# A decoder layer's shared expert: its last units in blocks of 512 tokens instead of 256

## The chip, the cores and the metric

The kernel runs on one core of a Trainium2 chip. The metric is device time in microseconds (us) of one execution. The engines are named as in the profile: PE (TensorE matmuls), PEld (TensorE weight loads), DVE (VectorE), ACT (ScalarE), POOL (GpSimd) and SP (SyncE, which issues most DMA transfers).

## The reference

One pre-norm decoder layer over x of 2 x 2048 tokens with 512 channels, all in float32:

```python
x = x + attn(layernorm(x))       # "attention" against two fixed matrices of 512 x 512, squared ReLU
x = x + xattn(layernorm(x))      # cross attention, 16 heads, 128 context rows, masked softmax
x = x + ffn(layernorm(x))

def ffn(h):                      # h: 4096 x 512
    shared = (silu(h @ sg) * (h @ su)) @ sd          # 512 -> 1024 -> 512, all tokens
    logits = h @ gate_w                              # 32 experts, the best one for each token
    e, s = argmax(logits), sigmoid(max(logits))
    xs = h * s
    routed = (silu(xs @ rg[e]) * (xs @ ru[e])) @ rd[e]
    return shared + routed
```

The change concerns `shared` alone, and of its 1024 hidden units only the last 256.

## The kernel before

Float32 products are made of three matmuls each. Every operand is split into a high part (a cast by ACT to the reduced type `fp32r`) and a low part (the difference, by DVE or POOL), and `three` lists low x high, high x low and high x high. So every weight or activation that comes from memory as `raw` costs one ACT cast and one DVE subtraction (`split`, L94 and L97) before PE can use it.

The layer goes through four stages. `stage0` is the first attention, `stage1` the cross attention and the routing scores. `stage1` also writes the normalised input of the feed-forward part, transposed and already split, to memory as `zT`: index 0 is the high part, index 1 the low part, then 128 partitions, 4 chunks k of 128 channels, and 4096 tokens in an order of its own (`place`). `shared` computes the first 768 hidden units of the shared expert. `routed` then computes the routed experts, and between their blocks the shared expert's last 256 units, which the class `Rest` holds.

`routed` sorts the experts by the number of their tokens into 32 ranks with fixed capacities:

```python
CAP = [448, 384] + [256] * 5 + [192] * 4 + [128] * 13 + [64] * 8
```

Its order takes one rank of over 128 rows, then one of 64 and one of 128, and so on, and two of 128 when those of 64 are used up. A rank is cut into blocks of 256, 128 or 64 rows. The list `blocks` mixes these with the blocks of `Rest`. Before the change, a `Rest` block has 256 tokens. The first stands ahead of everything, and one more follows each rank whose capacity isn't 128, until 15 are placed (behind ranks 0 to 7 and the seven ranks of 64 between them).

For block i the program writes, in this order: `prepare` of block i+2 (the gather of an expert's rows by POOL, or `Rest.load` by SP), the load of the next rank's gate weights (if this is the rank's last block), `first` (the gate product, or half of gate and up for 256 rows), the transposes of block i+1's rows, the transposes of block i-1's hidden rows, the load of the up weights, `second`, then `third` of block i-1 (its down product, and the store that adds it to the output) and the load of the down weights. The framework plans the final order of each engine from this order and its own estimate of the times, and each engine then follows its plan in order.

What limits the room: the pool W has 45 pieces of 128 x 512. The weights of `Rest` hold 12 of them and a rank's gate and up weights 32. The down weights use tags A and B. Raw weights pass through 6 slots of the pool `raw` and 8 of tag F. Tag E has 4 slots and serves the input z of `Rest`. PSUM has eight banks, two each under the tags P1 to P4. The tag I has two slots, for the rows v that go to the output. The names in the profile are L1107 (load of z), L1118 (gate and up of `Rest`), L1126, L1133, L1147 (down of `Rest`), L1150 and L1151 (copy and adding store of its rows), L1190 (raw weights), L1202 (gather), L1209, L1228 and L1308 (transposes), L1238 (blocks of 64 and 128 rows), L1293 and L1328 (blocks of 256 rows), L1336 (adding scatter of an expert's rows) and L1007 and L975 (the last of `shared`).

Of the kernel before, what the change touches and what calls it, by code (L numbers as in the profile page):

```python
# [8 lines left out]
F32 = mybir.dt.float32  # L9
FR = mybir.dt.float32r  # L10
# [4 lines left out]
A = mybir.AluOpType  # L15
AF = mybir.ActivationFunctionType
# [5 lines left out]
T = 4096  # L22
C = 512
E = 32
# [5 lines left out]
CAP = [448, 384] + [256] * 5 + [192] * 4 + [128] * 13 + [64] * 8  # L30
# [11 lines left out]
def f32(ap):  # L42
    return ap.bitcast(F32)


class Ctx:
# [4 lines left out]
    def __init__(self, tc, stack):  # L51
        self.tc, self.nc = tc, tc.nc
        enter = stack.enter_context
        self.c = enter(tc.tile_pool(name="c", bufs=1))
        self.sm = enter(tc.tile_pool(name="sm", bufs=3))
        self.raw = enter(tc.tile_pool(name="raw", bufs=6))
        self.W = enter(tc.tile_pool(name="W", bufs=45))
        self.a = enter(tc.tile_pool(name="a", bufs=1))
        self.ps = enter(tc.tile_pool(name="ps", bufs=2, space=PSUM))
# [29 lines left out]
def split(g, hi, lo, src, lo_engine=None, hi_engine=None):  # L89

    if isinstance(lo_engine, cycle):
        lo_engine = next(lo_engine)
    if hi_engine is None:
        g.nc.scalar.copy(hi, src)  # L94
    else:
        hi_engine.tensor_copy(hi, src)
    g.low = (lo_engine or g.nc.vector).tensor_tensor(lo, src, f32(hi), A.subtract)  # L97
# [22 lines left out]
def part(w, k, c):  # L120

    return w[k][c // 4][:, c % 4 * 128:c % 4 * 128 + 128]
# [40 lines left out]
def three(terms):  # L163

    (wh, wl), (xh, xl) = terms
    return (wl, xh), (wh, xl), (wh, xh)
# [199 lines left out]
def place(t):  # L366

    at = t // 4 * 4 + t % 2 * 2 + t % 4 // 2
    return slice(at * 256, at * 256 + 256)
# [723 lines left out]
class Rest:  # L1093


    def __init__(self, g, zT, out):
        self.g, self.zT, self.out = g, zT, out
        self.Z, self.S, self.H = {}, {}, {}

    def load(self, b):  # L1100
        g, nc = self.g, self.g.nc
        z = []
        for c in range(2):
            z.append([])
            for i in range(2):
                v = g.tile("E", "z", FR, (128, 2, 256))
                nc.sync.dma_start(f32(v[:]), self.zT[i, :, 2 * c:2 * c + 2, place(b)])  # L1107
                z[c].append(v)
        self.Z[b] = z

    def product(self, b, which, tag):
        g, nc = self.g, self.g.nc
        p = g.bank(tag, which, (128, 2, 256))
        for i in range(2):
            n = 0
            for k in range(4):
                for w, x in three((g.rest[which], self.Z[b][k // 2])):
                    nc.tensor.matmul(p[:, i, :], part(w, k, i), x[:, k % 2, :], start=n == 0, stop=n == 11)  # L1118
                    n += 1
        return p  # L1120

    def gate(self, b):
        g, nc = self.g, self.g.nc
        p = self.product(b, "g", "P2")
        s = g.tile("G", "s", F32, (128, 2, 256))
        nc.scalar.activation(s[:], p[:], AF.Silu)  # L1126
        self.S[b] = s

    def up(self, b):
        g, nc = self.g, self.g.nc  # L1130
        p = self.product(b, "u", "P3")
        s = self.S.pop(b)
        nc.vector.tensor_tensor(s[:], p[:], s[:], A.mult)  # L1133
        hh, hl = g.tile("C", "hh", FR, (128, 2, 256)), g.tile("D", "hl", FR, (128, 2, 256))
        split(g, hh[:], hl[:], s[:])
        self.H[b] = hh, hl
        del self.Z[b]

    def down(self, b):
        g, nc = self.g, self.g.nc  # L1140
        h = self.H.pop(b)
        for j in range(2):
            o = g.bank("P1", "d")
            n = 0
            for k in range(2):
                for w, y in three((g.rest["d"], h)):
                    nc.tensor.matmul(o[:], y[:, k, j * 128:(j + 1) * 128], w[k][0], start=n == 0, stop=n == 5)  # L1147
                    n += 1
            v = g.tile("I", "v")
            nc.scalar.copy(v[:], o[:])  # L1150
            nc.gpsimd.dma_start(self.out[b * 256 + j * 128:b * 256 + j * 128 + 128, :], v[:], accum_op=A.add)  # L1151

def routed(g, xs, rest, plan, idx, wg, wu, wd, out):
    nc = g.nc
    big = [r for r in range(E) if CAP[r] > 128]
    one = [r for r in range(E) if CAP[r] == 128]
    half = [r for r in range(E) if CAP[r] == 64]
    order = []  # L1160
    while big or one or half:
        few = half[:1] + one[:1] if half else one[:2]
        order += big[:1] + few
        big, one, half = big[1:], [r for r in one if r not in few], half[1:]
# [90 lines left out]
    def gate(b, r, m):  # L1255
        S[b] = []
        for n, p in enumerate(up_product(b, r, "g", "P2")):
            if m == 64:
                if n == 0:
                    S[b].append(g.tile("G", "s"))  # L1260
                both(S[b][0], p, n)
            else:
                s = g.tile("G", "s")
                nc.scalar.activation(s[:], p[:], AF.Silu)
                S[b].append(s)
        if m == 64:
            nc.scalar.activation(S[b][0][:], S[b][0][:], AF.Silu)

    def up(b, r, m):
        if m == 64:  # L1270
            u = g.tile("D", "u")
            for n, p in enumerate(up_product(b, r, "u", "P3")):
                both(u, p, n)
            s = S[b][0]
            nc.vector.tensor_tensor(s[:], u[:], s[:], A.mult)
            return
        for s, p in zip(S[b], up_product(b, r, "u", "P3")):
            nc.vector.tensor_tensor(s[:], p[:], s[:], A.mult)

    def hidden(b, r, part):  # L1280
        if part == 0:
            HT[b] = []
        for q in (2 * part, 2 * part + 1):
            o = []
            for which, tag in (("g", "P2"), ("u", "P3")):
                p = g.bank(tag, which, (128, 2, 256))
                for i in range(2):
                    cols = slice((2 * q + i) % 4 * 128, (2 * q + i) % 4 * 128 + 128)
                    n = 0
                    for k in range(4):  # L1290
                        piece = 2 * k + q // 2
                        for w, x in three((W[r][which], X[b][k // 2])):
                            nc.tensor.matmul(p[:, i, :], w[piece][:, cols], x[:, k % 2, :], start=n == 0, stop=n == 11)  # L1293
                            n += 1
                o.append(p)
            s = g.tile("G", "s", F32, (128, 2, 256))
            nc.scalar.activation(s[:], o[0][:], AF.Silu)
            nc.vector.tensor_tensor(s[:], o[1][:], s[:], A.mult)
            hh, hl = g.tile("C", "hh", FR, (128, 2, 256)), g.tile("D", "hl", FR, (128, 2, 256))
            split(g, hh[:], hl[:], s[:])  # L1300
            HT[b].append((hh, hl))
# [35 lines left out]
                                         in_=v[rows], in_offset=None, bounds_check=T - 1, oob_is_err=False, compute_op=A.add)  # L1337


    left = [(b, None, 256) for b in range(T // 256)]  # L1340
    blocks = [left.pop(0)]
    for r in order:
        at = 0
        while at < CAP[r]:
            m = next(m for m in (256, 128, 64) if at + m <= CAP[r])
            blocks.append((BASE[r] + at // 128, r, m))
            at += m
        if CAP[r] != 128 and left:
            blocks.append(left.pop(0))
    blocks += left  # L1350
    nxt = dict(zip(order, order[1:]))
# [7 lines left out]

    def first(b, r, m):  # L1360
        if r is None:
            rest.gate(b)
        elif m < 256:
            gate(b, r, m)
        else:
            hidden(b, r, 0)

    def second(b, r, m):
        if r is None:
            rest.up(b)  # L1370
        elif m < 256:
            up(b, r, m)
        else:
            hidden(b, r, 1)
# [7 lines left out]
    def turn_x(b, r, m, *tag):  # L1382
        if r is not None:
            turn(b, r, m, *tag)

    def turn_hidden(b, r, m):
        if r is not None:
            turn_h(b, r, m)
# [5 lines left out]
    for w in "gud":  # L1394
        load(order[0], w)
    for i, block in enumerate(blocks):
        b, r, m = block
        last = r is not None and (i + 1 == len(blocks) or blocks[i + 1][1] != r)
        if i + 2 < len(blocks):
            prepare(*blocks[i + 2])  # L1400
        if last and r in nxt:
            load(nxt[r], "g")
        first(*block)
        if i + 1 < len(blocks):
            turn_x(*blocks[i + 1])
        if i > 0:
            turn_hidden(*blocks[i - 1])
        if last and r in nxt:
            load(nxt[r], "u")
        second(*block)  # L1410
        if i > 0:
            third(*blocks[i - 1])
            r = blocks[i - 1][1]
            if r != block[1] and r in nxt:
                load(nxt[r], "d")
# [144 lines left out]
```

## Time and profile before

| what | value |
|---|---|
| median of 3 runs | 2699.37 us (2699.36 to 2700.18) |
| profiled execution, its own time | 2698.85 us |
| its span, first to last instruction | 2697.1 us |
| mean granted clock of PE | 0.996 |
| instructions of PE, busy share | 14629, 98% |
| gate and up of `Rest` (L1118) | 768 matmuls of 128 x 256, from 1789.8 us on; the last starts at about 2471 us |
| down of `Rest` (L1147) | 192 matmuls of 128 x 512 |
| loads of z for `Rest` (L1107) | 64 of 256 KB by SP |
| adding stores of `Rest` (L1151) | 32 of 256 KB by POOL |

A row of the profile's groups gives the line of the code, the engine, the operation, the output and the inputs, the shape, the count, the busy time and the mean time of one. A row of the timeline gives the start, the time and, in brackets, how long the engine stood idle before it and what ended that. Matmuls are pipelined, so one starts before the one ahead of it has ended, and the distance from start to start says more than the time of a row. A row of the windows gives a stretch, each engine's busy time and number of instructions in it, the granted clock, the busy share of the DMA engines and their GB/s.

### The profile page before, as it was taken

Reading aid. Unit: us, or ns where it says so; the run is one execution under the profiler, and the core shown is the slowest. Engines: PE = TensorE matmul, PEld = TensorE weight load, DVE = VectorE, ACT = ScalarE, POOL = GpSimd, SP = SyncE. Lnnn points to the kernel's source line nnn. Section 1 sums busy time; section 2 is a strip of 40 time slices with the busy share of each in tenths; the row PEclk is TensorE's granted clock in tenths of the full one; section 3 lists DMA queues with packets and bytes.
Section 4 is the critical chain, followed back from the end, with each engine's and each line's share of the span. In section 5 each row is a group of like instructions: output and inputs, shape, how many; then the busy total and the mean of one; then the engine's idle time right before and its main releaser. Section 6 shows DMA issues by size and latency. Waiting matters only on the chain. (4 is left out here: it accounts for less than half of the span.)

```text
span 2697.1 us, 47526 instructions
## 1 busy us (share of the span) xinstructions
PE 2639.6 (98%) x14629; PEld 2274.4 (84%) x14629; DVE 2033.8 (75%) x4559; ACT 1873.8 (69%) x4152; POOL 1129.3 (42%) x911
## 2 busy tenths in 40 slices
PE   7999999999999999999999999999999999999998
PEld 5878888887879999999987878778889898888886
DVE  7777777777777888888876596564776777778995
ACT  7788787888778877877874333333666777767885
POOL 5576566666654334444440547620122122212321
PEclk9999999999999999999999999999999999999999
DMA  4112112212020224232249846673899899999994
GB/s 154 32 63 87 55 67 81 77 43 83 30 86 27 87 76 138 96 108 90 102 158 327 273 140 239 223 214 109 260 287 276 279 302 292 299 280 291 325 324 142
DMA packets 269409, 446.68 MB, mean 166 GB/s; under 512 B 33536, under 2 KB 77568, under 8 KB 269152
## 3 DMA queue, kind: packets, MB, share of 16 engines
q1 hardware_dynamic: 254464, 416.46, 45.6%
q0 software_dynamic: 14688, 27.17, 5.1%
q8 instruction: 116, 1.90, 0.3%
q14 instruction: 141, 1.16, 0.1%
HBM read 348.83 MB, written 96.64 MB: 165 GB/s over the span
## 5 line engine op out<-in xcount | busy, mean ns | idle before, releaser
L97 DVE TENSOR_TENSOR rl<-raw,rh 128x512 fp32r<-128x512 f32 x768 | 488.2, 683 | 90.6 <-ACT rh L94 64.0
L94 ACT CAST rh<-raw 128x512 fp32r<-128x512 f32 x768 | 438.3, 621 | 141.6 <-DMA raw<-in_rg 98.2
L97 POOL TENSOR_TENSOR pl<-p,ph 128x512 fp32r<-128x512 f32 x320 | 411.4, 1297 | 264.3 <-ACT ph L94 210.0
L349 ACT ACTIVATE rl<-s 128x512 f32<-128x512 f32 x512 | 293.2, 604 | 38.2 <-PE s L345 30.6
L1336 POOL DMA_INDIRECT out_dram<-v,idx x46 | 114.2, 2483 | 463.6 <-ACT v L1334 368.7
L470 POOL TENSOR_TENSOR e<-e,ri 128x512 f32<-128x512 f32 x128 | 132.8, 1043 | 305.8 <-DVE ri L468 159.4
L353 DVE TENSOR_TENSOR p<-s,rl 128x512 f32<-128x512 f32 x320 | 215.1, 683 | 41.7 <-ACT rl L349 39.1
L94 ACT CAST ph<-p 128x512 fp32r<-128x512 f32 x320 | 199.2, 626 | 60.1 <-DVE p L353 57.4
L467 ACT ACTIVATE e<-e,mn 128x128 f32<-128x128 f32 x512 | 199.9, 392 | 27.9 <-DVE mn L462 26.7
L345 PE MATMUL s<-qh,kwl 128*128 128x512 f32 x512 | 205.5, 403 | 6.4 <-DVE p L353 3.1
L309 PE MATMUL o<-pl,vwh 128*128 128x512 f32 x512 | 203.1, 397 | 2.2 <-POOL pl L97 2.2
L353 DVE TENSOR_TENSOR s<-s,rl 128x512 f32<-128x512 f32 x192 | 133.3, 694 | 91.2 <-ACT rl L349 90.8
L309 PE MATMUL o<-ph,vwl 128*128 128x512 f32 x512 | 200.9, 394 | 1.0 <-ACT ph L94 1.0
L345 PE MATMUL s<-ql,kwh 128*128 128x512 f32 x512 | 200.3, 391 | 0.0
L345 PE MATMUL s<-qh,kwh 128*128 128x512 f32 x512 | 200.1, 391 | 0.0
L309 PE MATMUL o<-ph,vwh 128*128 128x512 f32 x512 | 199.6, 390 | 0.0
L975 PE MATMUL gu<-z,swh 128*128 128x512 f32 x504 | 158.3, 392 | 0.0
L440 PE MATMUL q<-yh,wql 128*128 128x256 f32 x512 | 147.3, 288 | 1.5 <-ACT yh L94 0.6
L97 DVE TENSOR_TENSOR pl<-s,ph 128x512 fp32r<-128x512 f32 x192 | 131.1, 683 | 21.1 <-ACT ph L94 18.6
L440 PE MATMUL q<-yh,wqh 128*128 128x256 f32 x512 | 146.3, 286 | 0.0
L440 PE MATMUL q<-yl,wqh 128*128 128x256 f32 x512 | 145.9, 285 | 0.0
L345 PEld LDWEIGHTS s<-qh,kwl 128*128 128x128 f32 x512 | 96.6, 189 | 33.1 <-DVE p L353 8.6
(361 smaller groups left out, 7958.0 us busy)
## 6 DMA issues: line engine op xcount, KB each, us to landing
raw<-in_rg SPq DMA_DIRECT2D x256, 256.0 KB, 5.4
raw<-in_ru SPq DMA_DIRECT2D x256, 256.0 KB, 5.4
raw<-in_rd SPq DMA_DIRECT2D x256, 256.0 KB, 5.3
z<-zT SPq DMA_DIRECT2D x116, 256.0 KB, 5.6
b<-x SPq DMA_DIRECT2D x40, 256.0 KB, 3.0
raw<-in_sgu SPq DMA_DIRECT2D x39, 256.0 KB, 4.2
swh<-wS SPq DMA_DIRECT2D x36, 256.0 KB, 4.9
swl<-wS SPq DMA_DIRECT2D x36, 256.0 KB, 4.9
```

What stands on the lines that cost most here:

```text
L94: g.nc.scalar.copy(hi, src)
L97: g.low = (lo_engine or g.nc.vector).tensor_tensor(lo, src, f32(hi), A.subtract)
L309: nc.tensor.matmul(o[:], w, y[:], start=kt == 0 and n == 0, stop=kt == 15 and n == 2)
L345: nc.tensor.matmul(s[:], w, y[:], start=n == 0, stop=n == 2)
L349: m0 = nc.scalar.activation(r[:], s[:], AF.Relu)
L353: m1 = nc.vector.tensor_tensor(p[:], s[:], r[:], A.mult)
L440: nc.tensor.matmul(o[:, i, :], part(w, k, p), y[k // 2][:, k % 2, :], start=n == 0, stop=n == 11)
L467: nc.scalar.activation(e[:, hs], e[:, hs], AF.Exp, bias=mn[:, h:h + 1], scale=-1.0, accum_out=su[:, h:h + 1])
L470: nc.gpsimd.tensor_tensor(e4, e4, ri[:].unsqueeze(2).to_broadcast([128, 4, 128]), A.mult)
L975: nc.tensor.matmul(o[:], y, z, start=(at, x) not in begun, stop=j == 1 and m == 2, skip_group_check=True)
L1336: nc.gpsimd.indirect_dma_start(out=out, out_offset=bass.IndirectOffsetOnAxis(ap=idx[rows, b + j:b + j + 1], axis=0), in_=v[rows], in_offse ...
```

## The change

`Rest` now has blocks of 512 tokens: 8 in place of 16. The input of a block is eight tiles of 128 x 512 (four chunks k, each with a high and a low part). `load` fetches the four high parts into the four slots of E and the first low part into a piece of W. The method `hidden` replaces `gate` and `up` and has two halves. The first half goes over the high parts: each meets the low and the high part of the gate and up weights, for both groups of 128 hidden units, in four PSUM banks that are open at the same time (P2 twice, P3 twice). As soon as a high part is used up, POOL fetches one of the other three low parts into its slot. The second half goes over the low parts, which meet the high parts of the weights, and then evicts the four banks: Silu, multiplication in PSUM, split. `down` makes four row groups of 128 tokens in a row, in P1 and P4 by turns.

The first block stands ahead of everything as before, but the transposes of the block after it now follow its second half. The other seven stand behind the ranks with a capacity over 128 and under 384, so behind ranks 2 to 8.

```diff
+    def part(self, b, i, k, engine, spare=False):
+        v = self.g.piece("z") if spare else self.g.tile("E", "z", FR)
+        engine.dma_start(f32(v[:]), self.zT[i, :, k, b * 512:(b + 1) * 512])
+        return v
+
     def load(self, b):
+        sp = self.g.nc.sync
+        self.Z[b] = [self.part(b, 0, k, sp) for k in range(4)] + [self.part(b, 1, 0, sp, True)]
+
+    def hidden(self, b, half):
         g, nc = self.g, self.g.nc
-        z = []
-        for c in range(2):
-            z.append([])
+        z = self.Z[b]
+        if half == 0:
+            self.S[b] = o = {}
             for i in range(2):
-                v = g.tile("E", "z", FR, (128, 2, 256))
-                nc.sync.dma_start(f32(v[:]), self.zT[i, :, 2 * c:2 * c + 2, place(b)])
-                z[c].append(v)
-        self.Z[b] = z
+                for which, tag in (("g", "P2"), ("u", "P3")):
+                    o[which, i] = g.bank(tag, which)
+        o = self.S[b]
+        for k in range(4 * half, 4 * half + 4):
+            if 0 < k < 4:
+                z.append(self.part(b, 1, k, nc.gpsimd))
+            for i in range(2):
+                for which in "gu":
+                    hi, lo = (part(w, k % 4, i) for w in g.rest[which])
+                    for n, w in enumerate((lo, hi) if k < 4 else (hi,)):
+                        nc.tensor.matmul(o[which, i][:], w, z[k][:], start=k == 0 and n == 0, stop=k == 7, skip_group_check=True)
+        if half == 0:
+            return
+        self.H[b] = []
         for i in range(2):
...
+            s, p = g.tile("G", "s"), o["u", i]
+            nc.scalar.activation(s[:], o["g", i][:], AF.Silu)
+            nc.vector.tensor_tensor(p[:], p[:], s[:], A.mult)
+            hh, hl = g.tile("C", "hh", FR), g.tile("D", "hl", FR)
+            split(g, hh[:], hl[:], p[:])
+            self.H[b].append((hh, hl))
 
     def down(self, b):
         g, nc = self.g, self.g.nc
         h = self.H.pop(b)
-        for j in range(2):
-            o = g.bank("P1", "d")
+        for s in range(4):
+            o = g.bank(("P1", "P4")[s % 2], "d")
             n = 0
             for k in range(2):
-                for w, y in three((g.rest["d"], h)):
-                    nc.tensor.matmul(o[:], y[:, k, j * 128:(j + 1) * 128], w[k][0], start=n == 0, stop=n == 5)
+                for w, y in three((g.rest["d"], h[k])):
+                    nc.tensor.matmul(o[:], y[:, s * 128:(s + 1) * 128], w[k][0], start=n == 0, stop=n == 5)
                     n += 1
             v = g.tile("I", "v")
             nc.scalar.copy(v[:], o[:])
-            nc.gpsimd.dma_start(self.out[b * 256 + j * 128:b * 256 + j * 128 + 128, :], v[:], accum_op=A.add)
+            at = (b // 2 * 4 + s // 2 * 2 + b % 2) * 256 + s % 2 * 128
+            nc.gpsimd.dma_start(self.out[at:at + 128, :], v[:], accum_op=A.add)
...
-    left = [(b, None, 256) for b in range(T // 256)]
+    left = [(b, None, 512) for b in range(T // 512)]
...
-        if CAP[r] != 128 and left:
+        if 128 < CAP[r] < 384 and left:
             blocks.append(left.pop(0))
...
         first(*block)
-        if i + 1 < len(blocks):
-            turn_x(*blocks[i + 1])
         if i > 0:
+            turn_x(*blocks[i + 1]) if i + 1 < len(blocks) else None
             turn_hidden(*blocks[i - 1])
         if last and r in nxt:
             load(nxt[r], "u")
         second(*block)
+        if i == 0:
+            turn_x(*blocks[1])
         if i > 0:
             third(*blocks[i - 1])
             r = blocks[i - 1][1]
```

`first` and `second` call `rest.hidden(b, 0)` and `rest.hidden(b, 1)` in place of `rest.gate(b)` and `rest.up(b)`.

More of the change, by code (lines that the diff above doesn't have):

```diff
@@ L1105, in load @@
             for i in range(2):
-                v = g.tile("E", "z", FR, (128, 2, 256))
-                nc.sync.dma_start(f32(v[:]), self.zT[i, :, 2 * c:2 * c + 2, place(b)])
-                z[c].append(v)
-        self.Z[b] = z
-    def product(self, b, which, tag):
-        g, nc = self.g, self.g.nc
-        p = g.bank(tag, which, (128, 2, 256))
-        for i in range(2):
[L1115 to L1137, printed above, removed]
+                for which, tag in (("g", "P2"), ("u", "P3")):
+                    o[which, i] = g.bank(tag, which)
@@ L1361, in first @@
         if r is None:
-            rest.gate(b)
+            rest.hidden(b, 0)
         elif m < 256:
@@ L1369, in second @@
         if r is None:
-            rest.up(b)
+            rest.hidden(b, 1)
         elif m < 256:
```

## The prediction

> **What bounds the kernel now.** I read the page first (the chain view of this run holds only the last 8 us, so it settles nothing about the changed stage), then the windows, PE's waits, the instruction rows around the edited lines, and the DMA issues of the stage.
>
> ```profile
> PE 2639.6 (98%) x14629; PEld 2274.4 (84%) x14629; DVE 2033.8 (75%) x4559; ACT 1873.8 (69%) x4152; POOL 1129.3 (42%) x911
> ...
> 1789.00:2688.00 899.00, 889.86 (x5079) 777.74 (x5077) 666.71 (x1089) 609.30 (x1138) 196.77 (x123) 1.00 0.85 269
> ...
> 1850.00:1900.00 50.00, 50.00 (x261) 42.76 (x260) 32.63 (x53) 30.04 (x57) 8.10 (x6) 1.00 0.68 202
> 2050.00:2100.00 50.00, 49.90 (x275) 42.96 (x274) 34.73 (x58) 33.40 (x63) 12.35 (x9) 1.00 0.93 287
> 2550.00:2600.00 50.00, 50.00 (x240) 41.52 (x238) 45.13 (x75) 44.08 (x84) 13.75 (x6) 1.00 0.92 312
> ```
>
> The first line is the page's, the others are windows (columns PE, PEld, DVE, ACT, POOL, granted clock, DMA share, GB/s). All that the change touches lies in the second: from the shared expert's last units (1789) to the end of the routed experts (2688). A busy PE is not yet a full PE, so I check its pitch, start to start:
>
> ```profile
> 2104.27 0.39 PE L1147 MATMUL d<-rdl,hh 128*128 128x512 f32 x1
> 2104.49 0.39 PE L1147 MATMUL d<-rdh,hl 128*128 128x512 f32 x1
> 2104.72 0.39 PE L1147 MATMUL d<-rdh,hh 128*128 128x512 f32 x1
> 2104.95 0.28 PE L1293 MATMUL g<-th,rl 128*128 128x256 f32 x1
> 2105.06 0.28 PE L1293 MATMUL g<-tl,rh 128*128 128x256 f32 x1
> 2105.18 0.28 PE L1293 MATMUL g<-th,rh 128*128 128x256 f32 x1
> 2105.30 0.28 PE L1293 MATMUL g<-th,rl 128*128 128x256 f32 x1
> ```
>
> Rows last 0.39 and 0.28 us, but starts follow every 0.227 us (512 columns) and 0.120 us (256). PE's waits in the stage add up to some 8 us; the stage is a stream of matmuls at these pitches, with DMA at 0.85 and VectorE at 0.74 behind it. So a matmul saved here is time saved, and a PE wait added is time lost: nothing else hides it.
>
> ```profile
> 1803.95 0.66 PE L1209 MATMUL pt<-ident,x 128*128 128x128 f32 x4 [2.70 <-DMA x<-xs,idx]
> ...
> 1805.53 0.63 PE L1007 MATMUL d<-dwl,hh 128*128 128x512 f32 x1
> 1805.96 0.63 PE L1007 MATMUL d<-dwh,hl 128*128 128x512 f32 x1
> 1806.39 0.63 PE L1007 MATMUL d<-dwh,hh 128*128 128x512 f32 x1
> ```
>
> This is the stage's one real hole: PE's queue stands 2.70 us at transposes whose gathered rows have not landed, and just after it eight matmuls run at a pitch of 0.43 (half clock).
>
> **The change part by part.**
>
> *Width.* 16 blocks of 256 tokens had 48 matmuls each for gate and up: 768 x 0.120 = 92.2 us. Eight blocks of 512 have 48 each: 384 x 0.227 = 87.2. Minus 5.0 us, all on the path. The Trainium skill (TensorE: Matmul & The Clock Gate, "Wait — 56ns, not 53.3ns?") puts the fixed cost of a matmul at about 2.5 ns beside its columns; by that, 384 fewer would save 1.0 us. The rows say 2 x 0.120 - 0.227 = 13 ns a pair; I take the rows. Going round four banks costs nothing: g and u of two banks alternate at 0.12 in L1293. The down products (192 x 0.227), 16 Silus, multiplies, splits and 32 copies of v stay as many and as wide; that some now read PSUM costs nothing while ACT and VectorE have a quarter free (without that cover, some 10 ns each, under 1 us).
>
> *Start.* The first block's 512 tokens keep PE at gate and up for 384/8 = 48 x 0.227 = 10.9 us in place of 5.8, and the transposes that caused the 2.70 us hole are moved behind its second half. Hole, half clock (8 x 0.2 = 1.6) and the 1.1 us wait for a P4 bank just after come to 5.4 us. Against it, the first half wants both P2 and both P3 banks at once, and the shared expert's last evictions free P3 only about 1795, while ready down products last from 1788 to about 1794. Bounds: gain 5.4, loss 2; I take -3, nearer to the gain because the new work is just what was missing there. The first block's low parts are covered by the shared expert's remaining down products.
>
> *Low parts of z.* Now the new wait. High parts fill the four E slots and one low part the spare W piece (12 + 32 of 45 are taken), loaded two blocks ahead as before. Low parts 1 to 3 can only be issued once high parts 0 to 2 are used up, from POOL's queue:
>
> ```profile
> z<-zT SPq DMA_DIRECT2D x57, 256.0 KB, 6.2
> out_dram<-v POOLq DMA_DIRECT2D x32, 256.0 KB, 6.9
> out_dram<-v,idx POOLq DMA_INDIRECT x46, 8.1
> x<-xs,idx POOLq DMA_INDIRECT x43, 6.7
> ...
> L1151 POOL DMA_DIRECT2D out_dram<-v x32: 882/985/1308, 1809.9 to 2492.1; - x32
> ...
> L1336 POOL DMA_INDIRECT out_dram<-v,idx x46: 1428/1954/5507, 1859.5 to 2687.7; - x46
> ```
>
> (the last number of the first four: us from issue to landing). Count from the first matmul of a middle block. Each k of the first half is 8 x 0.227 = 1.8 us, so slots come free at 1.8, 3.6 and 5.4. POOL just then still has the scatter of the block before the previous one, whose matmuls ended at 0: copy 0.6, hand-over, 2.0 of issue, so POOL is free at about 3.0, then 1.0 a load. Issues at 3.0, 4.0, 5.6; landing takes 6.4 (between z's own 6.2 from SP and the gather's 6.7 from POOL): there at 9.4, 10.4, 12.0. PE: first half done at 7.3, four small transposes 0.4, k=4 (the spare piece) to 8.6. It waits 0.8 for low part 1, 0.1 for 2, 0.7 for 3: 1.6 us a block, seven blocks: +11.2 us. Behind PE then wait the second half and the previous rank's down products (up to 48 x 0.227 = 10.9 us), which would have been ready: they cover the wait only if the planned order puts them ahead of the second half. The hole at 1804 speaks against that: there PE's order trusted a gather (issued 1797.61, landed about 1803.9) too early though down products were ready. The skill (DMA: Bandwidth & Descriptors, "Anatomy of one DMA — SWDGE (gpsimd) path") has 2.0 us + bytes/436e3, so 2.6 us for 256 KB: the last would land at 8.2, before it is wanted, and the term would be 0. The rows of this stage say 6.2 and 6.7; I use them. Bounds 0 and 25.
>
> *Eviction of the down product.* A block's four copies of v now go through two I slots in a row, every 6 x 0.227 = 1.4 us. The third needs the first's store landed (0.6 + 1.0 of POOL + 6.9), so ACT, in order, can stand 5 us. Behind it are casts of the next weights, VectorE's subtractions, and then PE. PE has 24 matmuls (5.4 us) on weights already split, and the four P1/P4 banks hold the results. Bounds 0 and 1 us a block; +1 in all. The stores follow earlier ones into the same output as before.
>
> *Queues and DMA.* SP loses 24 loads net (64 to 40), POOL gains 24 x 1.0 us at 22% busy. The rows of z double to 2 KB, the bytes stay. DMA is at 0.85, and both it and SP run ahead of PE: 0. Covered by PE; without cover, a few us.
>
> *Places.* The 15 blocks stood behind ranks 0 to 7 of over 128 rows and after the 64-row ranks among them; the seven stand behind ranks 2 to 8. Ranks 0 and 1 have 448 and 384 rows of their own work and DMA at 0.68 there; from rank 2 on work per loaded byte is what it was, and ranks 9, 21, 22, 10, 23 run like the uncovered tail now, which loses nothing at 2550. 0, bounds -1 and +3.
>
> Sum: -5.0 - 3 + 11.2 + 1 = +4.2 on the profiled execution's 2698.85 us (span 2697.1 and 1.75 around it): 2703.0. It lay 0.5 under the median 2699.37, so 2703.5.
>
> **Rivals.**
> *The wait is filled (faster).* The planned order puts the previous rank's down products, or part of them, before the late k. For: this order does weave streams elsewhere, as in the first block's g and L1007 at 1790; against: the hole at 1804. Then -5.0 - 3 + 1 = -7: 2692.4.
> *POOL's queue is the clock (slower).* Where POOL issues low part 1 later than about 5 us (a scatter that waits for an earlier store, as "POOL out_dram L1151 <- DMA out_dram<-v,idx", 44.8 us over 8 times, shows), or landing takes 8 under DMA 0.9, each block stands about 3.5 us: 7 x 3.5 = 24.5, sum +17.5: 2716.9. Past some 2.7 us in one piece the half clock could follow, as at 1805, by 1.6 more each.
> *It does not do what it says.* If four open banks drop the pitch gain, the sum is +9: within the first two's span.
>
> **How the numbers follow.** Waits as worked out 0.45, filled 0.30, POOL late 0.25. 0.2%, 5.4 us, is about what a measurement of this kernel can tell from no change: 2694.0 to 2704.8. The first case (own range 2698 to 2709) gives same 0.26, slower 0.18, faster 0.01; the second faster 0.25, same 0.05; the third slower 0.23, same 0.02. Predicted 2703.5; range 2690 to 2717.
>
> **What would show it.** PE and PEld at 14245; blocks of z at a pitch of 0.227; POOL 935. Right: PE waits "<-DMA z<-zT" of 1 to 2 us between k=4 and k=7 of seven blocks, and no 2.70 at the first transposes. Filled: L1238 or L1328 down products between the halves, no z wait. Wrong altogether: PE waits for weights (rl) or a bank in ranks 0 and 1, or a scatter row on POOL ahead of each z load.

## The result and the profile after

| kernel | median, us | ratio to before, 95% interval |
|---|---|---|
| before (same chip) | 2699.41 | |
| changed, 8 runs | 2708.8 | 1.0037 [1.0027, 1.0046] |
| changed, again in the last batch | 2712.72 | 1.0051 [1.0037, 1.0065] |

The change costs 0.37%, some 10 us (7 to 12 by the interval), where the prediction had +4. The profiled execution has a span of 2708.0 us against 2697.1. These are the page's first line of the changed kernel, and the windows of the changed stage (columns as in the prediction):

```profile
PE 2638.8 (97%) x14245; PEld 2250.9 (83%) x14245; DVE 2028.6 (75%) x4559; ACT 1869.3 (69%) x4152; POOL 1158.0 (43%) x935
...
1789.00:2699.00 910.00, 889.69 (x4694) 755.00 (x4692) 662.39 (x1088) 604.55 (x1138) 224.99 (x146) 1.00 0.84 265
...
2050.00:2100.00 50.00, 47.44 (x298) 42.20 (x297) 40.53 (x67) 36.53 (x70) 8.93 (x9) 1.00 0.96 309
```

The counts are as forecast: 384 matmuls fewer, 24 POOL instructions more. The stage takes 910 us in place of 899. PE waits 12 us longer in it, and its busy time is the same 889.7 us, although the wider matmuls should have taken 5 us off it (experiment 3 comes back to that). The window from 2050 shows the waits, 47.4 of 50 us busy where it was 49.9. PE's waits in this stage (us in total, times, longest), of the changed kernel:

```profile
PE g L1126 <- DMA z<-zT: 7.0, 4, 4.7
PE pt L1228 <- ACT v L1149: 5.5, 4, 2.0
PE u L1293 <- DVE rl L97: 3.4, 4, 0.9
```

All of the stage's listed PE waits add up to 19.4 us; before, they came to 7.5 us, of which 2.7 for the gathered rows at the start. That line is gone. Three new ones stand in its place: a wait for the low parts of z (L1126 is now the gate and up product), a wait for a PSUM bank that the copies of v (L1149) hold, and a wait for the weights of the next large rank. Their rows, around the first middle block. First POOL's timeline:

```profile
2022.31 4.14 POOL L1336 DMA_INDIRECT out_dram<-v,idx  x1 [14.50 <-DMA raw<-in_rd]
2025.90 2.33 POOL L1103 DMA_DIRECT2D z<-zT  x3
```

The block's first matmul starts at 2021.25. The slots of the first two high parts are free at about 2023.1 and 2024.9, but POOL stands in a scatter until 2025.9 and then issues the three loads in one go. PE's first matmul on a low part that POOL fetched starts at 2034.43, 8.5 us later. In between it works off, among others, 14 down products of the previous rank, so most of the delay is covered and 1.07 us remain. Behind rank 8 the same thing goes worse, in PE's and POOL's timelines:

```profile
2531.53 0.40 PE L1126 MATMUL u<-z,rw 128*128 128x512 f32 x1
2536.64 0.80 PE L1126 MATMUL g<-z,rw 128*128 128x512 f32 x1 [4.71 <-DMA z<-zT]
2537.24 0.63 PE L1126 MATMUL u<-z,rw 128*128 128x512 f32 x1
2537.66 0.63 PE L1126 MATMUL g<-z,rw 128*128 128x512 f32 x1
...
2529.97 1.55 POOL L1336 DMA_INDIRECT out_dram<-v,idx  x1 [10.88 <-ACT v L1334]
2530.95 2.36 POOL L1103 DMA_DIRECT2D z<-zT  x3
```

There the loads stand behind a scatter that itself waits 10.88 us for a row v, and no down product stands in the gap: the planned order has 24 of them in the first half of this block and 8 behind the wait. PE stands for 4.71 us, and then runs at a pitch of 0.43 us instead of 0.227 for a while (half clock, as at 1805 before). The second new wait, in the timelines of ACT, POOL, DVE and PE about 40 us after the first block's start:

```profile
2054.64 0.58 ACT L1149 COPY v<-d 128x512 f32<-128x512 f32 x1
...
2057.61 0.59 ACT L1149 COPY v<-d 128x512 f32<-128x512 f32 x1 [1.88 <-DMA out_dram<-v,idx]
2058.09 2.71 ACT L94 CAST rh<-raw 128x512 fp32r<-128x512 f32 x5
2064.91 0.59 ACT L1149 COPY v<-d 128x512 f32<-128x512 f32 x1 [4.11 <-DMA out_dram<-v]
...
2058.05 1.87 POOL L1151 DMA_DIRECT2D out_dram<-v  x2 [6.50 <-DMA out_dram<-v,idx]
...
2066.05 1.29 DVE L97 TENSOR_TENSOR rl<-raw,rh 128x512 fp32r<-128x512 f32 x2 [4.20 <-ACT rh L94]
...
2067.53 0.66 PE L1228 MATMUL pt<-ident,x 128*128 128x128 f32 x4 [1.44 <-ACT v L1149]
...
2074.51 0.38 PE L1293 MATMUL u<-th,rl 128*128 128x256 f32 x1 [0.80 <-DVE rl L97]
```

The third copy of v needs a slot of I and so a landed store: ACT stands for 4.11 us. The first store was itself late: its copy ended at 2055.2, but POOL stood until 2058.05 for an earlier scatter to land, so some 2.8 of the 4.11 us come from there (an estimate from these two times). DVE stands for 4.20 us behind it, because no cast of a weight comes. The bank of the fourth row is still held when PE comes to the transposes of the next large rank, which use P4. And the up weights of that rank, whose casts stood behind the copy, are late by another 0.8 us at 2074.5. This picture repeats behind ranks 3, 4 and 5.

### The profile page after: what moved, and what is told of

The parts are those of the page before. It is cut to its first block, busy times and chain, and to the rows that moved or that the text cites. A ratio compares the mean times of both kernels' runs of the same rounds, so it can differ in the third digit from the quotient of the medians.

```text
span 2708.0 us, 46883 instructions
## 1 busy us (share of the span) xinstructions
PE 2638.8 (97%) x14245; PEld 2250.9 (83%) x14245; DVE 2028.6 (75%) x4559; ACT 1869.3 (69%) x4152; POOL 1158.0 (43%) x935
## 5 line engine op out<-in xcount | busy, mean ns | idle before, releaser
L1336 POOL DMA_INDIRECT out_dram<-v,idx x46 | 122.5, 2662 | 465.2 <-ACT v L1334 306.0
```

What stands on the lines that cost most here:

```text
L1336: nc.gpsimd.indirect_dma_start(out=out, out_offset=bass.IndirectOffsetOnAxis(ap=idx[rows, b + j:b + j + 1], axis=0), in_=v[rows], in_offse ...
```

## The experiments

The theory after these rows: two waits, each with its own cause (POOL's queue ahead of the z loads, two slots of I for four rows v), have eaten the gain of the width. The rivals: that the low parts come too late whoever loads them, and that the new places of the blocks make weights late. Every edit also makes the framework plan the order anew, so a difference of a few us can hold more than the edit itself. All ratios are to the kernel before, run on the same chip.

**1. Low parts by SP** (`e1_sp`)

```diff
-                z.append(self.part(b, 1, k, nc.gpsimd))
+                z.append(self.part(b, 1, k, nc.sync))
```

> The low parts 1 to 3 of z are issued by SP instead of POOL, nothing else. Theory (POOL's queue): in the changed kernel all three loads of a block leave POOL together, right behind a scatter of 3.5 to 4.1 us, up to 3 us after their slots came free, and land 8 us later; from SP each leaves when its slot is free, so PE's waits for z fall from 7.0 us (and 1.6 us of half clock behind the one of 4.7) to under 2, and the time from 2708.8 to about 2701. Rival (latency: the slot itself comes free too late): the waits stay above 5 us and the time at 2707 or more. Rival (SP's order): SP now stands for the slots with the weights behind it, waits for rl grow and eat the gain: 2705 to 2710.

Measured: 2701.28 us, ratio 1.0009 [1.0002, 1.0015], so 7.5 us less than the changed kernel's 2708.8 (7.6 by the ratios; experiment 9 says how far such differences between batches hold). SP issues the loads one by one, as slots come free, between loads of weights (SP's timeline of this kernel, at the first middle block):

```profile
2023.09 0.33 SPq L1103 DMA_DIRECT2D z<-zT  x1
2023.66 1.44 SPq L1190 DMA_DIRECT2D raw<-in_rg  x3
2025.21 0.38 SPq L1103 DMA_DIRECT2D z<-zT  x1
```

and PE's waits there are:

```profile
PE pt L1228 <- ACT v L1149: 3.6, 4, 1.5
PE u L1293 <- DVE rl L97: 3.4, 4, 0.9
PE ht L1209 <- ACT v L1149: 1.8, 1, 1.8
...
PE g L1126 <- DMA z<-zT: 0.6, 1, 0.6
```

The z wait falls from 7.0 to 0.6 us, and no half clock follows. The loads themselves land in 5.1 us (median). So it was the queue, and not the moment at which the slots come free. The waits for v and rl stay as they were.

**2. Four slots for v** (`e2_v`)

```diff
-            v = g.tile("I", "v")
+            v = g.tile("IG"[s % 2], "v")
```

> The four rows v of a block's down product go to two slots of I and two of G by turns, so that none waits for a store of the same block; the z loads stay with POOL. Theory (the slots of v): ACT's 27.2 us of waiting for out_dram<-v go, and with them PE's waits for the P4 bank (5.5 us at the transposes of the next big rank) and for rl at that rank's first matmuls (3.4 us, and what follows them): minus 8 to 12 us, 2697 to 2701. Rival (weights are late by the new places, not by ACT): only the P4 wait goes, rl waits stay at 3 to 4 us: about 2703.

Measured: 2701.61 us, 1.0013 [1.0005, 1.0022], 7.2 us less (6.5 by the ratios). ACT's line of the changed kernel that is gone, and PE's waits now:

```profile
ACT v L1149 <- DMA out_dram<-v: 27.2, 10, 5.3
...
PE g L1126 <- DMA z<-zT: 9.3, 5, 5.1
PE u L1293 <- DVE rl L97: 1.2, 2, 0.9
```

With it PE's wait for the P4 bank is gone (5.5 us), and the one for rl falls from 3.4 to 1.2. So these weights were late mainly because ACT stood at v, and the places are not their cause. The z wait grew by 2.3 us, which took a part of the gain back.

**3. Both** (`e3_both`, and again as `e11_both_again`)

> Both edits at once: low parts of z by SP, v in I and G by turns. Theory (two separate waits that add up): about 2708.8 - 8 - 10 = 2690, faster than before by 0.3%, which leaves the width's 5 us and the start's 4. Rival (the waits stand in for each other, or SP's order takes the place): 2697 or more.

> The fast version again (low parts of z by SP, v in I and G by turns), beside the others of this batch on one chip: 2688 to 2691, ratio to before 0.995 to 0.998.

Measured: 2689.03 us, 0.9964 [0.9950, 0.9977], and again 2690.61 us, 0.9975 [0.9964, 0.9986]. This version beats both kernels. PE's waits of the first of them, the four longest:

```profile
PE d L1146 <- ACT hh L94: 1.5, 1, 1.5
PE g L1126 <- DMA z<-zT: 1.0, 1, 1.0
PE g L1293 <- ACT th L94: 0.8, 1, 0.8
PE d L1238 <- ACT th L94: 0.5, 1, 0.5
```

All of them add up to 5.2 us, against 19.4 in the changed kernel, and 13.7 and 13.4 in the two single edits. The time is about 20 us less than the changed kernel's, 6 more than the listed waits explain. The rest lies in PE's busy time. These are the windows of the stage, for this version, for its repeat, and for the one with matmuls of half the width (experiment 4):

```profile
1787.00:2677.00 890.00, 884.26 (x4693) 755.79 (x4692) 664.89 (x1088) 608.02 (x1139) 199.72 (x122) 1.00 0.85 271
...
1788.00:2678.00 890.00, 884.45 (x4696) 755.17 (x4694) 664.84 (x1089) 609.36 (x1139) 202.36 (x122) 1.00 0.85 271
...
1791.00:2687.00 896.00, 889.36 (x5079) 775.94 (x5077) 666.69 (x1090) 612.71 (x1139) 198.06 (x123) 1.00 0.85 269
```

Here PE is busy for 884.3 us, in the changed kernel for 889.7 with the same matmuls. Both have one stretch of half clock in the stage. So 5.4 us in the changed kernel are starts that come a little late, each too short to be listed as a wait; the busy time hides them. With both sums, 14.2 us of listed waits and 5.4 us of late starts, the 20 us are accounted for. Each single edit takes away about half of both sums (busy time 886.1 and 886.5 us). By the times the single edits gave 7.5 and 7.2 us, and the two together 20. How much of the 5 us above their sum is real cannot be told, since the changed kernel itself came out 4 us apart in two batches (experiment 9).

**4. The width alone** (`e5_half` on the changed kernel, `e10_both_half` on the version with both edits)

```diff
-                        nc.tensor.matmul(o[which, i][:], w, z[k][:], start=k == 0 and n == 0, ...)
+                        for c in (slice(0, 256), slice(256, 512)):
+                            nc.tensor.matmul(o[which, i][:, c], w, z[k][:, c], start=k == 0 and n == 0 and c.start == 0, ...)
```

> The changed kernel with each gate and up matmul of 512 columns issued as two of 256, same blocks, banks and waits: 384 matmuls more. By the pitches of the rows (0.120 and 0.227) this costs 384 x 13 ns = 5.0 us: about 2714. By the skill's fixed cost of 2.5 ns a matmul it costs 1.0 us: about 2710. If PE has slack in these blocks (other waits hide it): 2708 to 2709.

> Low parts of z by SP, v in I and G by turns, and each gate and up matmul of 512 columns as two of 256: the width alone taken out of the fast version. Theory (width is worth its pitch): 384 x 13 ns = 5.0 us over the fast version, so 2694. Rival (the 2.5 ns of the skill): 2690. Rival (as in the changed kernel, the shorter time of the rows lets waits grow): 2697 to 2699.

Measured: 2718.49 us, 1.0075 [1.0061, 1.0089], for the first, 10 us over the changed kernel and more than any of the three cases expected. PE's z wait grew to 9.2 us in it, and in its profiled execution (2725.0 us, the slowest of five) the half clock came in four places of the stage, so it says little about the width. Without these waits (5.0 us in all, 1.0 of it for z), the second gives 2696.94 us, 0.9993 [0.9984, 1.0001]. The version with both edits has 0.9975 [0.9964, 0.9986] on the same chip: the difference of 0.0018 is 4.9 us, the difference of the medians 6.3 us. The intervals just overlap, but the slowest of the seven runs with full width (2694.44) lies under the fastest of the thirteen without (2695.25), and PE's busy time in the windows above differs by 4.9 us (884.45 and 889.36). The width is worth what the pitches say (5.0 us). The 1.0 us that the prediction estimated from the fixed cost in the Trainium skill (TensorE: Matmul & The Clock Gate, "Wait — 56ns, not 53.3ns?") does not fit these matmuls.

**5. The moved transposes** (`e4_turn`)

```diff
         first(*block)
+        if i + 1 < len(blocks):
+            turn_x(*blocks[i + 1])
         if i > 0:
-            turn_x(*blocks[i + 1]) if i + 1 < len(blocks) else None
             turn_hidden(*blocks[i - 1])
...
-        if i == 0:
-            turn_x(*blocks[1])
```

> The changed kernel with the transposes of the first expert block put back between the halves of the first shared block, nothing else. Theory (the moved transposes closed the hole at the start): PE's wait for x<-xs,idx of 2 to 3 us and the half clock behind it return, 3 to 4 us: about 2712. Rival (512 tokens of work close it, the move was not needed): no such wait, 2708 to 2710.

Measured: 2710.02 us, 1.0047 [1.0034, 1.0060], against 1.0037 [1.0027, 1.0046] with the move: no difference that can be told. PE has no wait for `x<-xs,idx` in it either. The transposes (at 1803.70 there) come late enough by the longer first block alone.

**6. The places alone** (`e8_places`, `e12_single_start`), both in the kernel before, with its blocks of 256 tokens

```diff
-    blocks = [left.pop(0)]
+    blocks = [left.pop(0), left.pop(0)]        # e8_places alone
...
-        if CAP[r] != 128 and left:
-            blocks.append(left.pop(0))
+        if 128 < CAP[r] < 384 and left:
+            blocks += [left.pop(0), left.pop(0)]   # e12_single_start: as many as are left, up to two
```

> The kernel before, with its blocks of 256 tokens, its load, gate, up and down; only the places are the new ones: two blocks at the start and two in a row behind each of ranks 2 to 8. Theory (the places cost nothing in themselves, and the longer start closes the hole): 2694 to 2699, no waits for rl after the ranks of 64. Rival (the places themselves make the weights late): PE waits for rl of 3 us or more and 2703 to 2706. A wait of the second block of a pair for its z (its slots are those of the first) can add up to 1 us a pair.

> The kernel before with its blocks of 256 tokens, one at the start as before, two in a row behind each of ranks 2 to 8 and the last one behind rank 9: the new places without the longer start. Theory (the 7 us of the places are half start, half fewer small waits behind ranks 0 to 7 and the ranks of 64): the hole of 2 to 3 us at the first transposes and its half clock return, 2694 to 2696. Rival (all of it is the start): 2697 to 2699. Rival (the start adds nothing): 2691 to 2692.

Measured: 2691.05 us, 0.9972 [0.9962, 0.9982], and 2695.0 us, 0.9984 [0.9978, 0.9991]. PE's waits of the first:

```profile
PE g L1118 <- DMA z<-zT: 1.5, 2, 1.0
PE pt L1228 <- DVE acc L1013: 1.2, 1, 1.2
PE d L1238 <- ACT th L94: 0.5, 1, 0.5
PE d L1238 <- DVE tl L97: 0.2, 1, 0.2
```

and the second has, beside small ones, the old hole:

```profile
PE pt L1209 <- DMA x<-xs,idx: 2.7, 1, 2.7
```

So the new places are no cost but a gain, even without the wide blocks: 0.16% (4.3 us) for those behind the ranks. The second block at the start adds about 0.12% (3.2 us) by the medians, but these two intervals overlap and the runs are from different chips; that the start gains is shown by the rows (the hole of 2.7 us is there in the second and not in the first), its size only roughly. In `e8_places` PE waits for no weight and no bank between the start and the last rank. And its 0.9972 cannot be told from the 0.9964 and 0.9975 of the wide version with both edits: in the whole kernel, the new places with the old blocks of 256 tokens did as well as the best version with 512.

**7. Room elsewhere for the low parts** (`e7_early_v`), with v as in 2

```diff
-        v = self.g.piece("z") if spare else self.g.tile("E", "z", FR)
+        v = self.g.piece("z") if spare else self.g.tile("F" if i else "E", "z", FR)
...
-        self.Z[b] = [self.part(b, 0, k, sp) for k in range(4)] + [self.part(b, 1, 0, sp, True)]
+        self.Z[b] = [self.part(b, 0, k, sp) for k in range(4)] + [self.part(b, 1, k, sp, k == 0) for k in range(4)]
...
-            if 0 < k < 4:
-                z.append(self.part(b, 1, k, nc.gpsimd))
```

> v in I and G by turns, and all low parts of z loaded early with the high parts by SP: three of them in slots of F, which the raw weights use otherwise (11 in place of 14 slots for these while a block's input lies there). Theory (only the late issue of z matters, 3 slots of raw weights are to spare): no wait for z at all, 2686 to 2690, like or 1 to 2 us under the version with the loads by SP between the matmuls. Rival (raw slots are needed to keep DMA ahead at 0.85 to 0.95 busy): waits for rl take its place, 2692 or more.

Measured: 2713.3 us, 1.0057 [1.0045, 1.0070]: a miss, 24 us behind the version with loads by SP. PE has no wait for z, but the longest one in its list is

```profile
PE u L1291 <- DVE rl L97: 6.8, 7, 2.5
```

(L1291 is L1293 of the other kernels.) The weights are late in place of z. That this is for want of the three slots of F is the nearest reading; the order was planned anew as well, and I did not part the two. The waits are also not the whole of the 24 us: they add up to 18.0 us against 5.2, and in the profiled execution the half clock came in four places of the stage (from 2247 to 2251, for one, the mean granted clock was 0.57). Over the whole of each of its six executions it was 0.992 to 0.994, where the version with both edits had 0.996 to 0.998; what brought it there is open.

**8. Four slots for v in the kernel before** (`e9_before_v`), its two rows in I and G by turns

> The kernel before with its two rows v of a shared block in I and G by turns. Theory (two slots suffice for two rows, the wait is made by four in a row): same as before, 2697 to 2700, since ACT waited there only 11.3 us in all and PE not at all. Rival (the slots of v cost time before the change too): 2 us or more faster.

Measured: 2698.34 us, 0.9998 [0.9990, 1.0006]: the same. Two slots are enough for two rows: ACT stood 11.3 us for them in the kernel before, but no PE wait followed from it. The four rows in P1 and P4 made it a cost.

**9. The changed kernel again** (`e13_after_again`)

> The changed kernel again, unchanged, on the chip of this batch: 2707 to 2711, ratio to before 1.003 to 1.005. If it falls outside, the differences of the earlier batches need the same reserve.

Measured: 2712.72 us, 1.0051 [1.0037, 1.0065]. This is 2 us above the expected range, and 1.0051 lies above the 1.003 to 1.005 as well. The interval overlaps the first one; the changed kernel lies 10 to 14 us over before, and a difference of up to 4 us between batches is not to be read. So the 7.5 and 7.2 us of the single edits, which stand against the first batch, could be some 4 us more. The 20 us of both edits hold within the last batch too (1.0051 against 0.9975).

## Why the prediction was right or wrong, point by point

The measured +10 lies within the stated range and on the side forecast, but in part by luck: the places gained 4 us that stood at 0, and the eviction cost some 6 us more than its +1.

- *Bound by PE, every PE wait is time.* Right, with one addition. The sum of PE's waits and the time go the same way in the main kernels: 3.4 us of waits in `e8_places`, 5 with both edits, 7.5 before, 14 in the single edits, 19 in the changed kernel. But a wait is not the only loss: the changed kernel also has 5.4 us of late starts inside its busy time.
- *Width, -5.0.* Right, shown by `e10_both_half`: 4.9 by the ratios and 4.9 by the busy time.
- *Start, -3.* The size fits (about 3.2 us between the two kernels of experiment 6, not clear of the noise). The reason was half right: the longer block closes the hole, and the moved transposes add nothing.
- *Low parts of z, +11.2.* Measured: 7.0 us of waits and some 1.5 of half clock in the rows, 7.5 us by `e1_sp`. The size is near, but by luck, as a sum of two errors of opposite sign. POOL was later than I had it: at the first middle block the scatter ahead took 4.1 us and not 2.0, so the loads left at 4.7, 5.3 and 5.9 us after the block's start, and not at 3.0, 4.0 and 5.6. That is close to the 5 us at which the rival "POOL's queue is the clock" was to begin. And the rival "the wait is filled" was right about the order behind ranks 2 to 6: there 7 to 15 down products stand between the first low part and the first that POOL fetched, so these blocks waited for 1.07 us or less. Behind ranks 7 and 8 none stand there. The first of the two did not wait; at the second the slower rival came true in full, with 4.7 us and the half clock. The time to land that the rows give (8.5 us and 5.7 us from POOL's issue to the two waiting matmuls above, 5.1 from SP in the median) was the one to work with, and not the 2.6 us estimated from the Trainium skill (DMA: Bandwidth & Descriptors, "Anatomy of one DMA — SWDGE (gpsimd) path").
- *Eviction of the down product, +1.* This is the step that was furthest off. The mechanism was named, ACT standing for a store (5 us forecast, 4.11 in the row), but its price on PE was 5.5 us for the P4 bank and 2.2 of the 3.4 for late weights, 7.2 us by `e2_v`: as much as the bound of "1 us a block" would have given, of which I took a seventh. I counted the 24 matmuls that PE has ready and the four banks that hold the rows, and did not ask who needs P4 next: the transposes of the next large rank, which came 10 us after the last down product (at 2058.0 and 2067.5) and found the fourth row still in its bank.
- *Places, 0.* Wrong, and outside the bounds of -1 and +3: -4.3 us beside the start. I had looked for new waits only, and not at what the old places cost. The small waits of the kernel before for casts of the transposes and for products of the banks (2.1 us at L1293, 0.5 at L1147, 0.4) are absent from the list of `e12_single_start`, where two blocks of 256 stand together.
- *Queues and DMA, 0.* Right in the rows: DMA at 0.84, and no PE wait for a load that SP issued. The multiplies that now write PSUM took 690 ns in the median against 686 before (L1133), so that cost was nothing too.

The terms that single edits give, -5 (width), -3 (start), -4 (places), +7.5 (z) and +7 (v), add up to +2.5 against a measured +10. With the two waits taken as a pair, 20 us in place of 14.5, they add up to +8, which is within the interval of 7 to 12 us. So the sum closes to some 2 us for the pair; how the 20 us divide between the two waits stays open, within the 4 us by which the changed kernel differs between batches.

## What to carry to other kernels

When a kernel is one full stream on one engine, price a new wait by who stands next on each resource that it holds (the slot, the bank, the queue), and not only by the engine that waits: here ACT's stand of 4 us became PE time through a PSUM bank and through the casts behind it. A late load belongs in a queue whose own waits are short; the same three loads of each block cost 7.5 us less from SP than behind a scatter on POOL. And a change that bundles a new size with new places should be tried in parts: the new places and the longer start alone (0.28%) gave as much as the wide version at its best (0.25 to 0.36%), and the two waits that came with the size hid both gains.

## What the runs showed of the hardware that was not expected

- A scatter of POOL just ahead of the z loads took 3.5 to 4.1 us in five of the seven middle blocks (1.6 in the other two), against a median of 2.0 over all scatters of the kernel before. Why is open.
- The half clock follows a wait of PE in the middle of a dense stream, but the length of one wait does not tell when. It came (pitch 0.43) after 4.71 us in the changed kernel and after 2.70 us at 1804 before, but not after 1.99 us at 2152 in the changed kernel. It also came after 1.46 us in `e3_both` (1.00 us had been lost 5 us earlier), and not after 2.18 us in `e9_before_v`; first the rows of `e3_both`, then of `e9_before_v`:

```profile
1813.18 0.50 PE L1146 MATMUL d<-rdl,hh 128*128 128x512 f32 x1 [1.46 <-ACT hh L94]
1814.16 0.63 PE L1007 MATMUL d<-dwh,hl 128*128 128x512 f32 x1
1814.59 0.63 PE L1007 MATMUL d<-dwh,hh 128*128 128x512 f32 x1
...
1804.31 0.66 PE L1209 MATMUL pt<-ident,x 128*128 128x128 f32 x4 [2.18 <-DMA x<-xs,idx]
1805.04 0.39 PE L1007 MATMUL d<-dwl,hh 128*128 128x512 f32 x1
1805.27 0.39 PE L1007 MATMUL d<-dwh,hl 128*128 128x512 f32 x1
```

- 256 columns run at a pitch of 0.120 us and 512 at 0.227: 13 ns for each matmul more, in the rows and in the measured time of `e10_both_half`.
